# Splitting the evacuation of a products' bank, and a context in two column groups, in a two-layer metaformer kernel

## The chip, the cores and the metric

The kernel runs on one core of one Trainium2 chip. The metric is the device time of one execution in microseconds. Of the kernel before, three executions took 1307.3, 1311.6 and 1318.2 us, median 1311.6. One further execution was taken with the hardware profiler; all rows and durations below come from that one.

## The reference, cut to what matters

The input is x, 16 samples of 128 channels on 32 x 32 positions (1024 tokens), all in float32. Layer 0 adds linear attention and then a spectral filter (STU); layer 1 adds a pair of 3x3 convolutions and then a soft mixture of 64 experts. The change touches two places in layer 0: the attention's context, and the products of the spectral filter.

```python
q = jax.nn.softmax(q, axis=-2) * SCALE          # 4 heads of 32
k = jax.nn.softmax(k, axis=-1)
context = jnp.einsum('bhdc,bhec->bhde', k, v)
out = jnp.einsum('bhde,bhdc->bhec', context, q)
...
U_plus = jnp.fft.irfft(Vf[None, :, :, None] * Uf_p[:, :, None, :], n=n, axis=1)[:, :sl]
out = jnp.einsum('btkd,k,kde->bte', U_plus, s, Mpp)
out = out + jnp.einsum('btkd,k,kde->bte', U_minus, s, Mpm)
```

The second is a causal convolution over the 128 channels (the sequence of the filter is the channel axis) with 16 filters, each followed by a matrix; the same is done with a sign-alternated input. The kernel does it in the frequency domain: for every frequency it forms complex matrices G from filter spectra and mixed matrices, and multiplies the samples' spectra by it.

## The kernel before, in words

**Attention (about 10 to 395 us).** The work of a sample is cut into some 60 named steps. A table `period` lists the steps with a lag in samples, so that each pass over the table does steps of up to seven samples; this order is kept as written for TensorE, VectorE, ScalarE and GpSimd (a manual schedule pins these four; SP, which issues most DMAs, is ordered by the compiler). The step `context` (L476) multiplies, for each of 8 token tiles, the transposed exponentials of q (128 tokens x 128) by the scaled exponentials of k (128 x 128), and sums over the tiles in one PSUM tile `pc` of 128 x 128 (L482). All pairs of the four heads are computed, and `context_mask` (L488, VectorE) multiplies the result by a scale and a mask that keeps the four 32 x 32 blocks on the diagonal. Then `fold` and `fold2` combine it with output and value weights. PSUM tiles of a sample's 1024 numbers per partition come from `big`, three buffers. `moments` (L132) takes statistics of such a tile on VectorE; `tokens_copy` (L361), `input_copy` (L530) copy it to SBUF on ScalarE. `class_copy` (L232, L234) copies the upper half of a tile, `class_sums` and `class_differences` (L241, L248, L254) read its lower half on VectorE.

**Generation and products (about 395 to 676 us).** Frequencies are worked on in 16 chunks (NCH) of 8 (JL), with 128 columns each (CW). Two things happen per chunk:

- *Generation* of G for the next chunk, `generate(c, q)` (L774), in 8 parts q: each fills four PSUM banks, `pg[0]` to `pg[3]`, one for each group r of 32 rows, with four matrices of 128 columns. `collect` copies the four banks into the SBUF tile `g`, one bank per instruction, on VectorE (L785) or ScalarE (L787).
- *Products* with the present chunk, `multiply(c, m, x, py, fresh)` (L798): for each of four classes m and both halves x, 16 small matmuls write `py[:, x]`. `py` is one PSUM bank of 2 x 2 x 128 numbers per partition: x = 0 fills the first 256, x = 1 the second.

A float32 matmul appears as two TensorE instructions in the profile, so a generation part is 32 instructions and one half x of the products is 32.

The generations, the copies and the products of one m form a block; four blocks form a chunk. In a block, TensorE generates two parts (2m and 2m + 1) and then multiplies both halves. ScalarE then copies the whole bank `py` to the SBUF tile `yt` (L859), which has a single buffer. `combine` (L826, L827) adds and subtracts the two halves in SBUF on VectorE; it is called one block later, between the copies of the first part and those of the second. After the last class, `finish` (L812 to L815, GpSimd, in the last chunk VectorE) combines the classes and stores them (L819, SP). `begin(c)` (L765, L766 on GpSimd, loads L762 on SP) prepares the samples' spectra `v` of a chunk; it is called for the next chunk in the block m = 0, after `combine`.

`pg` and `py` share one pool, `psg`, of eight banks taken in turn. A block takes nine: four, four, one. So a block's `py` takes the bank that its own first `pg[0]` had, and the last bank of the next block's second generation is the one that `py` had.

**Convolutions and experts (about 688 us to the end).** Not touched.

Of the kernel before, what the change touches and what calls it, by code (L numbers as in the profile page):

```python
# [8 lines left out]
F32 = mybir.dt.float32  # L9
AF = mybir.ActivationFunctionType  # L10
ALU = mybir.AluOpType
# [3 lines left out]
P = 128  # L15
B, C, H, W = 16, 128, 32, 32
N = H * W
NT = N // 128
# [14 lines left out]
NCH = 16  # L33
JL = 8
# [6 lines left out]
RG = P // KR  # L41
# [25 lines left out]
def metaformer_kernel(ctx: ExitStack, tc: tile.TileContext, io: dict, out: bass.AP):  # L67
    nc = tc.nc
# [26 lines left out]
    for n, (g_, b_, m_, v_) in enumerate(((V_G1, V_B1, V_M1, V_V1), (V_G2, V_B2, V_M2, V_V2))):  # L95
# [15 lines left out]
                name=nc.get_next_instruction_name(), ins=[], outs=[], act_func_set_id=EXP_LN  # L111
# [52 lines left out]
    with ExitStack() as l0:  # L164
# [43 lines left out]
        with ExitStack() as a0:  # L208
# [8 lines left out]
            ps = a0.enter_context(tc.tile_pool(name="aps", bufs=2, space=PSUM))  # L217
# [97 lines left out]
            mask = aconst.tile([P, P], F32, name="mask")  # L315
            nc.vector.memset(mask, 0.0)
            for h in range(HEADS):
                s = slice(h * DH, (h + 1) * DH)
# [22 lines left out]
            class Attention:  # L341
# [134 lines left out]
                def context(self):  # L476


                    self.pc = ps.tile([P, P], F32, name="pc", tag="s")
                    ket = self.ke.rearrange("p (j h) d -> p j (h d)", h=HEADS)  # L480
                    for j in range(NT):
                        nc.tensor.matmul(  # L482
                            self.pc, self.qt[:, j, :], ket[:, j, :], start=(j == 0), stop=(j == NT - 1)
                        )

                def context_mask(self):
                    self.cx = work.tile([P, P], F32, name="cx", tag="cx")
                    nc.vector.scalar_tensor_tensor(  # L488
                        self.cx, self.pc, self.qs[:, 2:3], mask, ALU.mult, ALU.mult
                    )  # L490

                def fold(self):
# [253 lines left out]
        with ExitStack() as g0:  # L746
            gpl = [g0.enter_context(tc.tile_pool(name=f"gpl{i}", bufs=1)) for i in range(2)]
            cpl = g0.enter_context(tc.tile_pool(name="cpl", bufs=2))
# [5 lines left out]
            def begin(c):  # L754

                v = cpl.tile([P, 2 * NM * JL, 3, B], F32, name="v", tag="v")
                vs[c] = v
                vv = v.rearrange("p (x w) k b -> p x k b w", x=2)
                for i in range(B // BP):
                    bs = slice(i * BP, (i + 1) * BP)  # L760
                    xc = xcl.tile([P, BP, 2, 2, NM * JL], F32, name="xc", tag=f"xc{i}")
                    nc.sync.dma_start(xc.rearrange("p b x r w -> p b (x r w)"), vd[c, :, bs, :])  # L762
                    e, o = (xc[:, :, x].rearrange("p b r w -> p r b w") for x in range(2))
                    for x, op in enumerate((ALU.add, ALU.subtract)):
                        nc.gpsimd.tensor_tensor(vv[:, x, 1:, bs], e, o, op)  # L765
                    nc.gpsimd.tensor_scalar(v[:, :, 0, bs], v[:, :, 2, bs], -1.0, None, ALU.mult)  # L766
# [9 lines left out]
                        )  # L776
                return pg

            def collect(c, q, pg):

                for r in range(RG):
                    dst = gs[c].rearrange("p w (g q i) -> p g q w i", g=RG, q=NB)[:, r, q]
                    src = pg[r].rearrange("p i w -> p w i")
                    if r % 2 and (r == 1 or q % 4):
                        nc.vector.tensor_copy(dst, src)  # L785
                    else:
                        nc.scalar.copy(dst, src)  # L787

            def multiply(c, m, x, py, fresh):

                g, v = gs[c], vs[c]
                for kl in range(JL // RG):
                    for ri in range(2):
                        for grp in range(RG):
                            jl = RG * kl + grp
                            rows = slice(grp * 2 * B, (grp + 1) * 2 * B)

                            nc.tensor.matmul(  # L798
                                py[rows, x, kl, :],
                                v[:, (x * NM + m) * JL + jl, 1 - ri : 3 - ri, :]  # L800
                                .rearrange("p k b -> p (k b)"),
                                g[:, ((x * 2 + ri) * NM + m) * JL + jl, :],
                                start=(grp not in fresh), stop=(ri == 1), skip_group_check=True,
                            )
                            fresh.add(grp)
# [15 lines left out]
                        ys[:, kl].rearrange("p x m e -> p (x m e)"),  # L821
                    )

            def combine(c, m, ys, t):

                nc.vector.tensor_tensor(ys[:, :, 0, m], t[:, 1], t[:, 0], ALU.add)  # L826
                nc.vector.scalar_tensor_tensor(  # L827
                    ys[:, :, 1, m], t[:, 1], -1.0, t[:, 0], ALU.mult, ALU.add
                )
                if m == NM - 1:  # L830
                    finish(c, ys)

            with tc.manual_schedule(engines=PINNED):
                begin(0)
                gs[0] = gpl[0].tile([P, CW, C], F32, name="g", tag="g")
                for q in range(NB):
                    collect(0, q, generate(0, q))
                waiting = None
                for c in range(NCH):
                    if c + 1 < NCH:  # L840
                        gs[c + 1] = gpl[(c + 1) % 2].tile([P, CW, C], F32, name="g", tag="g")

                    ys = cpl.tile([P, JL // RG, 2, NM, C], F32, name="ys", tag="ys")
                    for m in range(NM):
                        if c + 1 < NCH:
                            pg = [generate(c + 1, 2 * m + x) for x in range(2)]
                            collect(c + 1, 2 * m, pg[0])
                        if waiting:
                            combine(*waiting)
                        if c + 1 < NCH:  # L850
                            if m == 0:
                                begin(c + 1)
                            collect(c + 1, 2 * m + 1, pg[1])
                        py = psg.tile([P, 2, JL // RG, C], F32, name="py", tag="p")
                        fresh = set()
                        for x in range(2):
                            multiply(c, m, x, py, fresh)
                        t = cpl.tile([P, 2, JL // RG, C], F32, name="yt", tag="yt", bufs=1)
                        nc.scalar.copy(t, py)  # L859
                        waiting = c, m, ys, t  # L860
                combine(*waiting)


    gpool = ctx.enter_context(tc.tile_pool(name="gpool", bufs=1))
# [9 lines left out]
    with ExitStack() as c1:  # L874
# [6 lines left out]
        ps = cps.enter_context(tc.tile_pool(name="cps", bufs=2, space=PSUM))  # L881
# [559 lines left out]
        with tc.manual_schedule(engines=PINNED):  # L1441
            hs, og = {}, {}
# [29 lines left out]
        ps = c1.enter_context(tc.tile_pool(name="fps", bufs=4, space=PSUM))  # L1472
        with tc.manual_schedule(engines=PINNED):
            for pr in (7, *range(NPAIR - 1)):
                py = [ps.tile([P, N], F32, name=f"pfy{j}", tag="pfy") for j in range(2)]
# [7 lines left out]
                for j in range(2):  # L1483
                    b = 2 * pr + j
                    if j and pr % 2:
                        t = first.tile([P, N], F32, name="yt", tag="v", bufs=2)
# [133 lines left out]
```

## Time and profile before

| | us |
|---|---|
| median of three executions | 1311.6 (1307.3 to 1318.2) |
| the profiled execution | 1324.2 |
| its span | 1322.4 |
| TensorE busy | 1209.1 (91%) |
| VectorE busy | 932.7 (71%) |
| ScalarE busy | 715.7 (54%) |
| GpSimd busy | 517.0 (39%) |
| chain that ended last: L774 | 9.1% of the span |
| chain: L798 | 8.2% |
| chain: L482 (context) | 2.2% |

In the rows, PE is TensorE, PEld its weight loads, DVE is VectorE, ACT ScalarE, POOL GpSimd, SP SyncE; L and a number is a line of the kernel. "us, us" in a timeline are the start from the span's beginning and the duration of a merged run of equal instructions; "xN" is how many. In brackets stands how long the engine had been idle before it and what ended that: an instruction of another engine, a DMA, or "issue", when nothing in the profile shows a reason. The chain of waits follows, from the last instruction back, what each step was released by. Shares of busy time are means over very different stages; what an edit in one stage is worth has to be read from that stage.

### The profile page before, as it was taken

To read this page: it belongs to the slowest core of one execution; us is meant where nothing else is said; L and a number is where in the kernel's file an instruction comes from. 1 tells how busy PE (TensorE), PEld (TensorE's weight loads), DVE (VectorE), ACT (ScalarE), POOL (GpSimd) and SP (SyncE) were. 2 spreads that over 40 slices of the span, in tenths; PEclk is the share of its full clock that TensorE was granted. 3 is DMA by queue.
4 is the path that set the end of the run, shared out by engine and by line. 5 is a ranking of instruction groups with operands and counts; after the bars stand their busy time and mean duration, and the time that the engine had idled before them with its cause. 6 is when DMAs were issued, how large, how long until landed. Compare 5 with 4: busy or idle time off the path is not lost.

```text
span 1322.4 us, 33679 instructions
## 1 busy us (share of the span) xinstructions
PE 1209.1 (91%) x14116; PEld 996.3 (75%) x14116; DVE 932.7 (71%) x1982; ACT 715.7 (54%) x1424; POOL 517.0 (39%) x816
## 2 busy tenths in 40 slices
PE   4889999999998999999938999999999999996875
PEld 3777777777767898898837988989889898872433
DVE  5688787887765778888747777777878777662224
ACT  3777777777546667666703345554545464652111
POOL 2324545454685888888832222121212121100002
PEclk8899999999998999999968999999999999995997
DMA  6014343433344333444375310312212113035986
GB/s 268 17 35 141 116 137 108 147 121 126 116 148 140 125 128 132 131 131 131 108 260 145 96 49 23 90 53 60 64 49 65 33 49 128 17 122 198 357 311 255
DMA packets 87400, 162.98 MB, mean 123 GB/s; under 512 B 5584, under 2 KB 40784, under 8 KB 86864
## 3 DMA queue, kind: packets, MB, share of 16 engines
q1 hardware_dynamic: 86608, 158.33, 36.1%
q0 software_dynamic: 640, 2.49, 0.6%
q8 instruction: 111, 1.82, 0.6%
q14 instruction: 41, 0.34, 0.1%
HBM read 104.18 MB, written 56.62 MB: 122 GB/s over the span
## 4 chain that ended last, share of the span: by engine, by line
PE 83%; DVE 6%; DMA 3%; ACT 3%; POOL 2%; issue 1%; SPq 0%; POOLq 0%; ACTq 0%; DVEq 0%
PE pcv L945 25%; PE pg L774 9%; PE py L798 8%; PE big L618 6%; PE big L149 4%; PE big L159 4%; PE big L1058 4%; PE big L551 3%; PE big L418 2%; PE pc L482 2%; PE big L514 2%; PE big L436 2%; DVE bst L132 2%; PE big L1206 1%; PE ph L1400 1%
## 5 line engine op out<-in xcount | busy, mean ns | idle before, releaser
L945 PE MATMUL pcv<-v,cw 128*128 128x256 f32 x1536 | 342.9, 380 | 0.0
L945 PEld LDWEIGHTS pcv<-v,cw 128*128 128x128 f32 x1536 | 286.8, 190 | 42.2 <-issue 5.7
L785 DVE COPY g<-pg 128x512 f32<-128x512 f32 x224 | 144.4, 682 | 60.6 <-PE pg L774 60.1
L787 ACT COPY g<-pg 128x512 f32<-128x512 f32 x288 | 147.3, 604 | 32.2 <-PE pg L774 32.1
L774 PE MATMUL pg<-ph,mst 32*128 32x128 f32 x4096 | 143.8, 279 | 4.1 <-issue 2.3
L774 PEld LDWEIGHTS pg<-ph,mst 32*128 32x128 f32 x4096 | 129.1, 186 | 19.8 <-issue 8.9
L798 PE MATMUL py<-g,v 128*32 128x128 f32 x4096 | 127.6, 276 | 9.3 <-POOL v L765 5.6
L798 PEld LDWEIGHTS py<-g,v 128*32 128x32 f32 x4096 | 110.1, 111 | 18.1 <-POOL v L765 5.8
L141 ACT ACTIVATE tok<-tok,sts 128x128 f32<-128x128 f32 x256 | 101.8, 481 | 23.8 <-POOL sts L1020 20.4
L132 DVE BATCH_NORM_STATS2 bst<-big 128x6 f32<-128x256 f32 x256 | 91.2, 418 | 19.1 <-PE big L154 12.1
L765 POOL TENSOR_TENSOR v<-xc 128x256 f32<-128x256 f32 x128 | 99.5, 801 | 9.3 <-DVE g L785 9.3
L1085 POOL TENSOR_SCALAR sts<-bst 128x8 f32<-128x8 f32 x16 | 6.5, 404 | 233.8 <-DVE bst L132 233.8
L939 DVE TENSOR_TENSOR v<-pads 128x544 f32<-128x544 f32 x128 | 85.0, 724 | 9.7 <-ACT pads L1138 9.3
L618 PE MATMUL big<-u,mu 128*128 128x128 f32 (+4 forms) x384 | 86.0, 380 | 0.0
L274 POOL TENSOR_TENSOR xf<-ab 128x256 f32<-128x256 f32 x34 | 24.8, 728 | 132.2 <-DVE ab L241 132.1
L859 ACT COPY yt<-py 128x512 f32<-128x512 f32 x64 | 37.5, 585 | 65.9 <-PE py L798 44.4
L618 PEld LDWEIGHTS big<-u,mu 128*128 128x128 f32 x384 | 56.7, 191 | 18.0 <-issue 15.4
L1116 ACT ACTIVATE ct<-pcv,bn 128x256 f32<-128x256 f32 x64 | 30.2, 473 | 69.3 <-PE pcv L945 68.4
L551 PE MATMUL big<-wf,ub 128*128 128x256 f32 x256 | 62.0, 385 | 0.2
L1134 DVE TENSOR_TENSOR r<-pcv,cs 128x256 f32<-128x256 f32 x64 | 27.0, 421 | 48.9 <-PE pcv L945 48.2
L149 PEld LDWEIGHTS big<-ident,x 128*128 128x128 f32 x384 | 47.3, 148 | 17.8 <-issue 7.2
L149 PE MATMUL big<-ident,x 128*128 128x128 f32 x384 | 53.8, 286 | 6.7 <-ACT tok L141 2.4
(231 smaller groups left out, 2341.5 us busy)
## 6 DMA issues: line engine op xcount, KB each, us to landing
we<-in_weight SPq DMA_DIRECT2D x32, 1024.0 KB, 11.1
vd<-xf SPq DMA_DIRECT2D x16, 1024.0 KB, 5.1
xc<-vd SPq DMA_DIRECT2D x64, 256.0 KB, 3.3
yd<-ys SPq DMA_DIRECT2D x32, 512.0 KB, 4.1
y<-yd SPq DMA_DIRECT2D x15, 896.0 KB, 6.5
x<-in_x SPq DMA_DIRECT2D x16, 512.0 KB, 4.1
mi<-in_M_phi SPq DMA_DIRECT2D x16, 512.0 KB, 5.0
xd<-x SPq DMA_DIRECT2D x16, 512.0 KB, 6.0
```

What stands on the lines that cost most here:

```text
L132: nc.vector.bn_stats(bst[:, j : j + 2, :].rearrange("p j s -> p (j s)"), src[:, j : j + 2, :].rearrange("p j c -> p c j"),)
L141: nc.scalar.activation(dst[:, j, :], src[:, j, :], AF.Identity, bias=nm[:, j : j + 1], scale=r[:, j : j + 1],)
L149: nc.tensor.transpose(pt[:, j, :], src[:, j * P : (j + 1) * P], ident)
L551: nc.tensor.matmul(dst, self.ub[:, q, :], wf[:, q, :], start=True, stop=True)
L618: nc.tensor.matmul(self.pa[:, a:hi], mu[:, NF - 1 - si, tap, :], self.u[:, a - tap : hi - tap], start=(tap == 0), stop=(tap == KU - 1),)
L765: nc.gpsimd.tensor_tensor(vv[:, x, 1:, bs], e, o, op)
L774: nc.tensor.matmul(pg[r][:, i], mst[rs, 4 * q + i, :], ph[rs, c, :], start=True, stop=True,)
L785: nc.vector.tensor_copy(dst, src)
L787: nc.scalar.copy(dst, src)
L798: nc.tensor.matmul(py[rows, x, kl, :], v[:, (x * NM + m) * JL + jl, 1 - ri : 3 - ri, :] .rearrange("p k b -> p (k b)"), g[:, ((x * 2 + ri) ...
L939: nc.vector.tensor_tensor(v[:, k], d[i], d[j], op)
L945: nc.tensor.matmul(pc[:, i], wt[:, dy, k, :], v[:, k, hf * HR + dy : hf * HR + dy + HR], start=(dy == 0), stop=(dy == 2),)
```

## The change

In the attention, the context is no longer 8 matmuls of 128 x 128 but 16: for each token tile, one for heads 0 and 1 (rows and columns 0 to 63) and one for heads 2 and 3 (64 to 127). Their outputs lie on partitions 0 to 63 and 64 to 127 of a PSUM tile of 128 x 64. The mask step reads that tile twice by a broadcast, so that the masked result has the same 128 x 128 numbers.

In the product stage,

- ScalarE copies only the first half of `py` (x = 0), between the two halves of the products, into a smaller `yt` with two buffers; the sums read the second half from PSUM;
- the sums of a block are issued at its own end, not in the next block;
- the copies of the generated banks alternate strictly: r = 0 and 2 on ScalarE, 1 and 3 on VectorE (before, ScalarE also had r = 3 for the parts 0 and 4);
- the copies of r = 2 and 3 of the second part are issued after the products;
- `begin` of the next chunk is called at the start of the chunk.

```diff
-                    self.pc = ps.tile([P, P], F32, name="pc", tag="s")
+                    self.pc = ps.tile([P, P // 2], F32, name="pc", tag="s")
...
                     for j in range(NT):
-                        nc.tensor.matmul(
-                            self.pc, self.qt[:, j, :], ket[:, j, :], start=(j == 0), stop=(j == NT - 1)
-                        )
+                        for g in range(2):
+                            hs = slice(g * P // 2, (g + 1) * P // 2)
+                            nc.tensor.matmul(
+                                self.pc[hs, :], self.qt[:, j, hs], ket[:, j, hs],
+                                start=(j == 0), stop=(j == NT - 1), skip_group_check=True,
+                            )
...
                     nc.vector.scalar_tensor_tensor(
-                        self.cx, self.pc, self.qs[:, 2:3], mask, ALU.mult, ALU.mult
+                        self.cx.rearrange("p (g e) -> p g e", g=2),
+                        self.pc.unsqueeze(1).to_broadcast([P, 2, P // 2]), self.qs[:, 2:3],
+                        mask.rearrange("p (g e) -> p g e", g=2), ALU.mult, ALU.mult,
                     )
...
-            def collect(c, q, pg):
+            def collect(c, q, pg, rs=range(RG)):
-                for r in range(RG):
+                for r in rs:
...
-                    if r % 2 and (r == 1 or q % 4):
+                    if r % 2:
                         nc.vector.tensor_copy(dst, src)
                     else:
                         nc.scalar.copy(dst, src)
...
-            def combine(c, m, ys, t):
-                nc.vector.tensor_tensor(ys[:, :, 0, m], t[:, 1], t[:, 0], ALU.add)
+            def combine(c, m, ys, py, t):
+                nc.vector.tensor_tensor(ys[:, :, 0, m], py[:, 1], t, ALU.add)
                 nc.vector.scalar_tensor_tensor(
-                    ys[:, :, 1, m], t[:, 1], -1.0, t[:, 0], ALU.mult, ALU.add
+                    ys[:, :, 1, m], py[:, 1], -1.0, t, ALU.mult, ALU.add
                 )
...
-                waiting = None
                 for c in range(NCH):
-                    if c + 1 < NCH:
+                    more = c + 1 < NCH
+                    if more:
                         gs[c + 1] = gpl[(c + 1) % 2].tile([P, CW, C], F32, name="g", tag="g")
+                        begin(c + 1)
                     ys = cpl.tile([P, JL // RG, 2, NM, C], F32, name="ys", tag="ys")
                     for m in range(NM):
-                        if c + 1 < NCH:
+                        if more:
                             pg = [generate(c + 1, 2 * m + x) for x in range(2)]
                             collect(c + 1, 2 * m, pg[0])
-                        if waiting:
-                            combine(*waiting)
-                        if c + 1 < NCH:
-                            if m == 0:
-                                begin(c + 1)
-                            collect(c + 1, 2 * m + 1, pg[1])
+                            collect(c + 1, 2 * m + 1, pg[1], range(2))
                         py = psg.tile([P, 2, JL // RG, C], F32, name="py", tag="p")
+                        t = cpl.tile([P, JL // RG, C], F32, name="yt", tag="yt")
                         fresh = set()
-                        for x in range(2):
-                            multiply(c, m, x, py, fresh)
-                        t = cpl.tile([P, 2, JL // RG, C], F32, name="yt", tag="yt", bufs=1)
-                        nc.scalar.copy(t, py)
-                        waiting = c, m, ys, t
-                combine(*waiting)
+                        multiply(c, m, 0, py, fresh)
+                        nc.scalar.copy(t, py[:, 0])
+                        multiply(c, m, 1, py, fresh)
+                        if more:
+                            collect(c + 1, 2 * m + 1, pg[1], range(2, RG))
+                        combine(c, m, ys, py, t)
```

## The prediction

> **What bounds the kernel now.** I read the page first, then the stage the change edits, then the second edit's place. The page's slices give the engine and the stages:
>
> ```profile
> PE   4889999999998999999938999999999999996875
> PEclk8899999999998999999968999999999999995997
> ```
>
> TensorE is nine tenths busy nearly everywhere. At 33.1 us a slice, slices 3 to 11 are attention and slices 12 to 20 (about 395 to 690 us) generation and products; the clock is full in both. The timeline of TensorE shows what a product block costs (one step of m: two generations, L774, then the products, L798):
>
> ```profile
> 545.44 2.07 PE L774 MATMUL pg<-ph,mst 32*128 32x128 f32 x64
> 547.44 1.95 PE L798 MATMUL py<-g,v 128*32 128x128 f32 x64
> 549.33 2.07 PE L774 MATMUL pg<-ph,mst 32*128 32x128 f32 x64
> ...
> 643.89 1.95 PE L798 MATMUL py<-g,v 128*32 128x128 f32 x64
> ...
> 659.75 1.96 PE L798 MATMUL py<-g,v 128*32 128x128 f32 x64
> 663.15 7.19 PE L798 MATMUL py<-g,v 128*32 128x128 f32 x256 [1.45 <-DVE pooled L868]
> ```
>
> An undisturbed block is 549.33 - 545.44 = 3.89 us: 2.00 generation, 1.89 products. The 60 blocks that start from 418.02 to 657.75 take 243.6 us (to 659.75 + 1.89), 4.06 each. So 0.17 x 60 = 10.2 us is all that faster evictions could return there; 3.4 of it are five TensorE gaps with no releaser ("issue", 1.06, 0.40, 0.45, 0.18 and 1.28 us), which I leave in place. 6.8 us can be won.
>
> The groups of instructions, shapes apart, give the engines that empty PSUM (count | busy us, mean ns | idle before):
>
> ```profile
> L787 ACT COPY g<-pg 128x512 f32<-128x512 f32 x288 | 147.3, 604 | 32.2 <-PE pg L774 32.1
> L785 DVE COPY g<-pg 128x512 f32<-128x512 f32 x224 | 144.4, 682 | 60.6 <-PE pg L774 60.1
> L827 DVE SCALAR_TENSOR_TENSOR ys<-yt 128x256 f32<-128x256 f32 x64 | 48.3, 755 | 0.0
> L859 ACT COPY yt<-py 128x512 f32<-128x512 f32 x64 | 37.5, 585 | 65.9 <-PE py L798 44.4 <-DVE ys L827 10.7 <-ACT g L787 8.5
> L826 DVE TENSOR_TENSOR ys<-yt 128x256 f32<-128x256 f32 x64 | 36.1, 565 | 4.4 <-POOL pads L924 2.2 <-ACT yt L859 2.2
> L361 ACT COPY tok<-big 128x1024 f32<-128x1024 f32 x16 | 16.2, 1013 | 14.9 <-DVE bst L132 5.4 <-PE big L149 4.8 <-PE pc L482 3.4
> ```
>
> Per block VectorE needs 3.5 x 682 + 565 + 755 = 3.7 us and ScalarE 4.5 x 604 + 585 = 3.3, both under 4.06: TensorE sets the pace. In attention the chain of waits shows one sample:
>
> ```profile
> 191.75 1.79 PE pc L482 x16
> ...
> 195.32 1.44 DVE bst L132 x4
> ...
> 196.84 1.02 ACT ub L530
> ...
> 197.90 1.09 PE big L159 x8
> ```
>
> The context, 1.79 us, lies on the path of every sample. The timeline shows what orders that ACT copy:
>
> ```profile
> 196.84 1.01 ACT L530 COPY ub<-big 128x1024 f32<-128x1024 f32 x1 [2.21 <-DVE bst L132]
> ...
> 206.18 0.60 ACT L234 ACTIVATE et<-big 128x512 f32<-128x512 f32 x1 [2.33 <-DVE ab L241]
> ```
>
> L530 and the bn_stats of L132 both only read the same PSUM tile, yet the copy starts when the statistics end. L234 reads the upper half of a tile (`pe[:, 2:]`) and L241 the lower half, and it too waits. Accesses to one PSUM tile by two engines are put one behind the other here, even reads of different halves.
>
> **The product block, part by part.** *The wait that is added.* The products' tile `py` is one bank of 512 numbers per partition. Now its first half is copied by ScalarE between the two halves of the products. By the two rows above, the second half's writes are queued behind that copy. TensorE then stands with nothing else to issue: its 32 instructions of x=1 wait, behind them the next block's generation, and behind that the copies of both evicting engines. The price: products are (1.95 - 0.27) / 63 = 26.7 ns apart (0.27 us is one instruction), so the last of the first 32 starts at 0.83 and ends at 1.10. ScalarE starts 0.11 later (products end at 645.84, the next L859 begins at 645.95). The copy of 256: from 585 ns for 512 and 1013 for 1024, 0.836 ns an element, so 0.37; bounds 0.31 (L118, 8 elements wide, 310 ns) and 0.47 (L1116, an ACTIVATE of 256 from PSUM, 473 ns). TensorE starts 0.05 after a ScalarE copy (L530 ends 197.85, L159 starts 197.90). Sum 1.63, where the second half used to start at 32 x 26.7 = 0.85: a stall of 0.78, bounds 0.72 and 0.88. ScalarE is free in time: its three earlier copies start 1.2, 1.7 and 2.2 after the block and end by 2.8, the half is ready at 2.00 + 1.10 = 3.10.
>
> The Trainium skill, "PSUM — Partial Sum Buffer", section "PSUM bank collisions raise a hardware error", speaks against this edit: guard PSUM by bank and quadrant, not by address, because two engines in one bank at once collide even at different columns. The trace agrees, with the waits of 2.21 and 2.33 us above; by address alone the sum would be that of the first rival below.
>
> *The sums.* L826 and L827 had two SBUF operands and ran 0.40 to 1.97 us beside a busy GpSimd. They now take one from PSUM, as L625 does in attention, whose 16 instances beside GpSimd stay between 1.224 and 1.226 us. L1124 and L1125 have this shape with one PSUM operand: 419 and 413 ns. I take 0.77 for the pair (672.00 to 672.77 undisturbed). It is now at the block's end, ahead of the next block's VectorE copies: it starts at 2.00 + 1.63 + 1.10 + 0.11 = 4.84 and ends at 5.61, while the next block starts at 3.89 + 0.78 = 4.67, its first copies at 4.67 + 1.2 = 5.9. The bank it frees is needed by the fourth tile of that block's second generation, at 4.67 + 1.00 + 0.19 = 5.86. It costs nothing, with 0.2 us to spare.
>
> *The evictions.* 32 copies go from ScalarE to VectorE. VectorE then has 4 x 682 + 770 = 3.5 us, ScalarE 4 x 604 + 371 = 2.8, of 4.67. The 6.8 us of bank stalls go, since these come from the sums pushing L785 back. ScalarE's third copy of the second generation, now behind the half copy, ends at 3.57 + 0.6 = 4.2; its bank is needed at 5.7: hidden.
>
> *The moved start of the next values* (GpSimd L765, L766 and four loads on SP). Order on GpSimd and SP is as before: last chunk's L812 to L815 and its stores, then these. GpSimd has 4.2 + 10.2 = 14.4 us of work in a chunk that grows to 18.7; it stays hidden.
>
> Sum: 60 x (3.89 + 0.78) + 3.4 = 283.6 against 243.6, +40.0. First block +0.8. Last chunk, four blocks of products only, +3.1. The wait of 1.5 us ahead of it (661.64 to 663.15, for GpSimd's values) goes: -1.5. Behind the last product, today's backlog of single-buffered copies and sums ends 6.0 us later (670.34 to 676.38); now 0.11 + 0.77 and L812 to L815 on VectorE (674.17 to 676.38, 2.2) make 3.1: -2.9. Stage: **+39.5**.
>
> **The context.** 16 instructions 112 ns apart become 32 with half the columns, in two column groups. Nearest row:
>
> ```profile
> 835.59 1.97 PE L1261 MATMUL pp<-tt,gtt 128*64 128x128 f32 x32
> ```
>
> Two groups of 64, 128 moving columns: (1.97 - 0.27) / 31 = 54.8 ns apart. Around it TensorE loses 0.10 in front (835.59 less 832.90 + 12 x 0.216) and 0.15 behind (837.49 less 835.59 + 32 x 0.0548), 0.25 in all, which a plain context doesn't pay. Lower bound: the products' 26.7 ns, 32 x 0.0267 + 0.25 = 1.10, -0.69. Upper bound: 54.8 stays, if loading weights sets it: 2.00, +0.21. I take half of 54.8, 27.4 ns, since L1261's spacing is that of its moving columns shared by two groups (L945 shows 216 ns per 256): 1.13, -0.66. The bn_stats wait behind moves along with TensorE (it idles 0.75 for L154). 14 of the 16 samples are on the path; the first two run into a wait of 2.88 us for VectorE (74.48). **-9.2**; at the upper bound +2.9.
>
> The page "TensorE: Matmul & The Clock Gate" ("LDWEIGHTS") gives columns / 1.2 ns for a weight load, 53 ns for 64, and in its Part 3 lets loads overlap running matmuls only across row groups; by that the context would take 32 x 0.053 + 0.25 = 1.96 us, about +2.3 in all. The products' 26.7 ns, across column groups, don't decide it, as their loads are 32 wide.
>
> The mask (L488, 351 ns) keeps its element count.
>
> **Total**: +39.5 - 9.2 = +30.3. On the profiled execution, 1324.2 us (span 1322.4), that is 1354.5; on the median of the runs, 1311.6, it is **1342**. With the upper bound for the context, 1354.
>
> **Rivals.**
> 1. *No wait in mid-block: faster.* If dependencies are kept by address, x=1 runs on. Then 6.8 + 1.5 + 2.9 us return and the context's 9.2: -20, **1291**. For it: the halves don't overlap. Against: L234, whose half doesn't overlap either. It decides if the stall is under about 0.3 us (0.3 x 65 = 20).
> 2. *VectorE becomes the bound as well.* If the sums still stretch to 0.95 each beside GpSimd, the pair ends at 4.84 + 1.6 = 6.4, 0.6 past the 5.86 at which the bank is needed: 60 x 0.6 = +36 more, **1378**. Against: L625.
> 3. *The context doesn't overlap*: **1354**, still slower.
>
> **How the numbers follow.** Forecast 0.50; rival 3, 0.32; rival 1, 0.09; rival 2, 0.05; between forecast and rival 1, 0.04. About 1% is what a measurement tells from no change (1298 to 1325). Faster by over 1%: 0.09. Within: 0.05. Slower: 0.86. Forecast and rival 3 alone, with stalls of 0.72 to 0.88 us over 65 blocks (-4, +7) and the 3.4 us of gaps hidden or not, reach from 1335 to 1361; the run spread (1307 to 1318) adds some 5 each way. Range 1326 to 1366.
>
> **What would show it.** Right: every L798 run split in two groups of 32 with 0.7 to 0.9 us of TensorE idle between, released by ACT's yt copy; blocks 4.6 to 4.8 us apart; L826 and L827 near 0.42 us; TensorE about 83% busy at full clock there (as at 60 to 80 us, 15.98 of 20 us, clock 1.00). Context: 32 instructions in 1.1 to 1.2 us. Wrong: 64 products without a gap (rival 1); gaps inside L774 released by VectorE (rival 2); a context of 2 us (rival 3); a clock below full in the stage, which I haven't priced.

## The result, and the profile after

| | before | after |
|---|---|---|
| median of four executions, us | 1312.6 (1307.3 to 1318.2) | 1353.6 (1350.2 to 1358.9) |
| ratio, 95% interval | | 1.0298 (1.0261 to 1.0334) |
| the profiled execution, us | 1324.2 | 1350.8 |
| its span, us | 1322.4 | 1349.1 |

The change costs 41 us in the medians, 26.7 us between the spans of the two profiled executions. Every ratio in this document is against executions of the kernel before that were taken along; their median was 1312.6 us here and 1315.8 to 1317.3 us beside the experiments, so ratios compare better than microseconds. The lines have moved by five (generation is L779 now, products L803), the sums are L831 and L832, the context is L484.

The page's slices of the changed kernel, TensorE's busy share and granted clock:

```profile
PE   4889999999978888888883999999999999996886
PEclk9999999999999999999996899999999999997998
```

In slices 13 to 19 (counted from 0), all of the product stage, TensorE's share has fallen from 9 to 8, at a granted clock of 1.00 (413 to 690 us): TensorE stands, it isn't slowed. The timeline of one block with its second half, sums and half copy shows where:

```profile
540.01 2.23 PE L779 MATMUL pg<-ph,mst 32*128 32x128 f32 x64
540.22 0.42 DVE L831 TENSOR_TENSOR ys<-py,yt 128x256 f32<-128x256 f32 x1 [1.28 <-PE py L803]
540.56 0.41 DVE L832 SCALAR_TENSOR_TENSOR ys<-py,yt 128x256 f32<-128x256 f32 x1
...
542.17 1.08 PE L803 MATMUL py<-g,v 128*32 128x128 f32 x32
543.37 0.37 ACT L859 COPY yt<-py 128x256 f32<-128x256 f32 x1 [0.60 <-ACT g L792]
...
543.79 1.08 PE L803 MATMUL py<-g,v 128*32 128x128 f32 x32 [0.54 <-ACT yt L859]
...
544.80 2.32 PE L779 MATMUL pg<-ph,mst 32*128 32x128 f32 x64
```

The products' run of 64 has become two of 32. Between them lie 0.54 us that ScalarE's copy of `yt` ends. The first 32 start at 542.17, the second at 543.79, so the products take 2.63 us to the next generation at 544.80, where they took 1.89. The generation, too, is longer: 2.16 us from 540.01 to 542.17, where an undisturbed one took 2.00. The block is 544.80 - 540.01 = 4.79 us, which is also the median of the stage, against 3.89 undisturbed before. The average before was 4.13: the 243.6 us that the prediction divides by 60 hold 59 blocks (more on this below).

The waits in the stage, summed (us in total, times, longest):

```profile
PE py L803 <- ACT yt L859: 32.3, 60, 0.8
...
PE pg L779 <- issue: 2.2, 4, 1.1
```

Sixty waits for the half copy, one in each block with a generation. The groups of the copies show how long their engines now stand:

```profile
L792 ACT COPY g<-pg 128x512 f32<-128x512 f32 x256 | 139.0, 592 | 116.7 <-PE pg L779 115.5
...
L790 DVE COPY g<-pg 128x512 f32<-128x512 f32 x256 | 159.4, 684 | 18.9 <-PE pg L779 18.6
```

ScalarE stood 32.2 us ahead of these copies before and stands 116.7 now. VectorE's idle time has moved: 60.6 us ahead of its copies before and 18.9 now, but now 62.6 us ahead of the sums, for the products. In the stage, ScalarE's busy share fell from 68% to 50% and VectorE's from 78% to 66%: both have room that nobody uses, since TensorE feeds them more slowly.

In attention, the chain of waits of the changed kernel for the sample that was shown before:

```profile
185.41 1.08 PE pc L484 x32
186.49 1.02 PE big L159 x8
...
188.43 1.44 DVE bst L132 x4
...
189.95 1.02 ACT ub L535
```

Before, the line behind the context was:

```profile
193.53 0.87 PE big L159 x8
```

The context has gone from 1.79 to 1.08 us with twice the instructions. The transposes behind it (L159) went from 0.87 to 1.02, so the sample gains 0.56.

The timeline of TensorE at the end of the stage:

```profile
708.12 1.08 PE L803 MATMUL py<-g,v 128*32 128x128 f32 x32 [0.54 <-ACT yt L859]
723.32 1.20 PE L1060 MATMUL big<-wi,y 128*128 128x128 f32 x4 [14.12 <-DMA y<-yd]
```

The wait between last product and first convolution product is 14.12 us; it was 17.34.

To compare runs I cut each profiled span at four events that every kernel has: the first context product, the first generation, the last product of the spectral filter, the first product of the convolutions.

| us | to context | attention | stage | wait behind it | rest |
|---|---|---|---|---|---|
| before | 55.1 | 340.2 | 275.1 | 17.3 | 634.7 |
| after | 52.5 | 332.3 | 324.4 | 14.1 | 625.8 |
| difference | -2.6 | -7.9 | +49.3 | -3.2 | -8.9 |

The change touches the middle three: +38.2 us. The first and the last column hold work that no kernel here alters, and they vary from execution to execution: over the twelve profiles of this study the first runs from 51.7 to 55.5, the last from 625.8 to 636.7. In the one of before, the granted clock was 0.84 from 5 to 35 us and 0.96 over 600 us of the last part; in the one of after 0.90 and 0.97. That profile of before was a long execution of its kernel, which is why the spans show less than the medians do.

### The profile page after: what moved, and what is told of

The parts are those of the page before. It is cut to its first block, busy times and chain, and to the rows that moved or that the text cites. A ratio compares the mean times of both kernels' runs of the same rounds, so it can differ in the third digit from the quotient of the medians.

```text
span 1349.1 us, 34300 instructions
## 1 busy us (share of the span) xinstructions
PE 1208.9 (90%) x14372; PEld 982.7 (73%) x14372; DVE 925.0 (69%) x2014; ACT 687.7 (51%) x1392; POOL 505.2 (37%) x816
## 4 chain that ended last, share of the span: by engine, by line
PE 81%; DVE 5%; ACT 5%; DMA 3%; issue 3%; POOL 1%; SPq 0%; POOLq 0%; ACTq 0%; DVEq 0%
PE pcv L947 24%; PE pg L779 10%; PE py L803 8%; PE big L623 6%; PE big L159 4%; PE big L149 4%; PE big L1060 4%; PE big L556 3%; PE big L436 2%; PE big L418 2%; PE big L519 2%; DVE bst L132 2%; ACT yt L859 2%; PE big L1208 1%; PE pp L1263 1%
## 5 line engine op out<-in xcount | busy, mean ns | idle before, releaser
L792 ACT COPY g<-pg 128x512 f32<-128x512 f32 x256 | 139.0, 592 | 116.7 <-PE pg L779 115.5
L803 PE MATMUL py<-g,v 128*32 128x128 f32 x4096 | 139.5, 278 | 41.9 <-ACT yt L859 34.5
L790 DVE COPY g<-pg 128x512 f32<-128x512 f32 x256 | 159.4, 684 | 18.9 <-PE pg L779 18.6
L803 PEld LDWEIGHTS py<-g,v 128*32 128x32 f32 x4096 | 105.2, 110 | 67.2 <-ACT yt L859 51.9
L779 PE MATMUL pg<-ph,mst 32*128 32x128 f32 x4096 | 148.7, 281 | 4.0 <-issue 2.2
L779 PEld LDWEIGHTS pg<-ph,mst 32*128 32x128 f32 x4096 | 135.6, 187 | 18.3 <-issue 17.7
L770 POOL TENSOR_TENSOR v<-xc 128x256 f32<-128x256 f32 x128 | 91.3, 738 | 9.8 <-DMA xd<-x 9.8
L831 DVE TENSOR_TENSOR ys<-py,yt 128x256 f32<-128x256 f32 x64 | 27.2, 425 | 98.7 <-PE py L803 67.7
L623 PEld LDWEIGHTS big<-u,mu 128*128 128x128 f32 x384 | 56.7, 191 | 18.0 <-issue 15.4
L1118 ACT ACTIVATE ct<-pcv,bn 128x256 f32<-128x256 f32 x64 | 30.3, 474 | 67.5 <-PE pcv L947 66.6
```

The source lines that it names most:

```text
L623: nc.tensor.matmul(self.pa[:, a:hi], mu[:, NF - 1 - si, tap, :], self.u[:, a - tap : hi - tap], start=(tap == 0), stop=(tap == KU - 1),)
L779: nc.tensor.matmul(pg[r][:, i], mst[rs, 4 * q + i, :], ph[rs, c, :], start=True, stop=True,)
L803: nc.tensor.matmul(py[rows, x, kl, :], v[:, (x * NM + m) * JL + jl, 1 - ri : 3 - ri, :] .rearrange("p k b -> p (k b)"), g[:, ((x * 2 + ri) ...
```

## The experiments

Two things needed a cause: the gap in mid-products, and the 0.16 us by which the generation had grown, which I hadn't foreseen. For the gap the theory (A in the expectations) is that the second half's writes wait for a copy out of the same bank; the rival is that 32 small matmuls with a gap are simply how this split runs. For the generation the theory (B in the expectations) is that the bank which the sums release comes too late for the generation's last tile; the rival is that generation became slower for a reason of its own, such as VectorE reading PSUM beside it. A third cause came up in the first runs, late instruction fetches (C).

**One bank for each half (e1).** Each half gets a tile of its own, and with it a bank of its own; products and sums address `py[0]` and `py[1]`. Against the changed kernel:

```diff
-                        py = psg.tile([P, 2, JL // RG, C], F32, name="py", tag="p")
+                        py = [psg.tile([P, JL // RG, C], F32, name="py", tag="p") for x in range(2)]
...
-                        multiply(c, m, 0, py, fresh)
-                        nc.scalar.copy(t, py[:, 0])
-                        multiply(c, m, 1, py, fresh)
+                        multiply(c, m, 0, py, set())
+                        nc.scalar.copy(t, py[0])
+                        multiply(c, m, 1, py, set())
```

> The changed kernel with the two halves of the products in two PSUM banks instead of one. Theory A (the second half's products are queued behind ScalarE's copy because both are in one bank): the 0.54 us TensorE gap in the middle of every products run vanishes, 64 products run in 1.95 us again, a block takes 2.16 + 1.89 = 4.05 us instead of 4.79; over 60 blocks -44 us, with the last chunk -46: about 1307 us, ratio to the kernel before 0.995 (0.99 to 1.00). The generation's 0.16 us over 2.00 stays (theory B: its last tile waits for the bank that the sums free). Rival (the gap comes from splitting the products into two runs, or from ScalarE being late, not from the shared bank): the gap stays, 1345 to 1360 us, ratio about 1.03.

Measured: 1327.7 us (1320.2 to 1331.3), ratio 1.0077 (1.0043 to 1.0111). The timeline of that kernel, TensorE and one half copy:

```profile
545.83 1.95 PE L803 MATMUL py<-g,v 128*32 128x128 f32 x64
547.02 0.37 ACT L858 COPY yt<-py 128x256 f32<-128x256 f32 x1 [0.60 <-PE py L803]
...
547.71 2.40 PE L779 MATMUL pg<-ph,mst 32*128 32x128 f32 x64
...
550.04 1.95 PE L803 MATMUL py<-g,v 128*32 128x128 f32 x64
...
551.92 1.61 PE L779 MATMUL pg<-ph,mst 32*128 32x128 f32 x45
...
554.41 0.93 PE L779 MATMUL pg<-ph,mst 32*128 32x128 f32 x19 [0.88 <-issue]
```

With the same copy at the same place, 64 products run in 1.95 us without a gap. So the gap comes from what the two halves shared, and not from the split: that is shown. Whether it is the bank or the tile isn't: e1 separates both at once, and a tile of two banks wasn't tried. A row of the prediction points at the tile: L234 reads the second 512 numbers of a tile of 1024 and L241 the first 512, so by the 512 numbers of a bank they read different banks, and yet L234 waited 2.33 us for L241.

The time didn't follow: the ratio is 1.0077 where 0.995 was expected, some 17 us more. The last line shows the kind of thing that ate it: TensorE stops inside a generation and no engine and no semaphore released it. Between the starts of two matmuls inside generations there are 22 gaps of over 0.25 us in this run, 17.3 us in all, where the kernel before had 10 with 5.4 and the changed one 8 with 4.8. What they follow is told with e7.

**The half copy behind both halves, one bank (e2).** Against the changed kernel:

```diff
                         multiply(c, m, 0, py, fresh)
-                        nc.scalar.copy(t, py[:, 0])
                         multiply(c, m, 1, py, fresh)
+                        nc.scalar.copy(t, py[:, 0])
```

> The changed kernel with ScalarE's copy of the first half issued after both halves of the products, still one bank. Theory A: no gap inside the products. Theory B (the generation is stretched because the bank of the products is freed only when both sums have read it): the sums now end about 0.42 us later, 1.38 us after the generation's start instead of 0.96, so the generation grows from 2.16 to about 2.6 us, all of it at the fourth tile of its second part; block 4.5 us, 60 x -0.3 = -18 and the last chunk -3: about 1333 us, ratio 1.015. Rival to B (the generation's 0.16 us has another cause, for instance evictions on both engines at once): the generation stays at 2.16, block 4.05, about 1309 us, ratio 0.997.

Measured: 1340.3 us (1338.2 to 1344.7), ratio 1.0193 (1.0167 to 1.0218). The timeline of that kernel:

```profile
571.39 1.95 PE L803 MATMUL py<-g,v 128*32 128x128 f32 x64
...
573.27 2.71 PE L779 MATMUL pg<-ph,mst 32*128 32x128 f32 x64
573.45 0.37 ACT L860 COPY yt<-py 128x256 f32<-128x256 f32 x1 [1.58 <-PE py L803]
...
573.86 0.42 DVE L831 TENSOR_TENSOR ys<-py,yt 128x256 f32<-128x256 f32 x1 [1.24 <-ACT yt L860]
574.20 0.41 DVE L832 SCALAR_TENSOR_TENSOR ys<-py,yt 128x256 f32<-128x256 f32 x1
...
575.91 0.32 PE L803 MATMUL py<-g,v 128*32 128x128 f32 x4
```

The products are whole again. The sums now wait for the copy and end at 574.61, 1.34 us into the generation, which grows to 2.64 (575.91 - 573.27; median of the run 2.60). The stall has moved from the products into the generation: the later the bank is released, the longer the generation. That is what B says. It is also why a copy at the end is no repair by itself: the block is 4.48 us. The ratio was expected at 1.015; this run, too, has more gaps without a releaser, 18 with 13.2 us.

**The second sum without the bank (e6).** The second sum is formed in SBUF as twice the first half less the first sum, so that the bank is free after the first sum; the result is the same difference, rounded otherwise. Against the changed kernel:

```diff
                 nc.vector.scalar_tensor_tensor(
-                    ys[:, :, 1, m], py[:, 1], -1.0, t, ALU.mult, ALU.add
+                    ys[:, :, 1, m], t, 2.0, ys[:, :, 0, m], ALU.mult, ALU.subtract
                 )
```

> The changed kernel with the second sum taken from SBUF, as twice the copied half less the first sum, so that only the first sum reads the products' bank. Theory B (the last tile of the next generation waits, with its weight load, for the bank that both sums hold until 0.96 us into the generation; without a wait that load would start at about 0.9): the bank is free at 0.63, the generation falls from 2.16 to 2.00 us, the block from 4.79 to 4.63, 60 x -0.16 = -9.6: about 1344 us, ratio 1.023. The second sum, now with both operands in SBUF, may stretch to 0.95 us beside GpSimd; VectorE has room for it. Rival (another cause of the 0.16): the generation stays at 2.16, 1353, ratio 1.030.

Measured: 1341.9 us (1338.5 to 1344.4), ratio 1.0191 (1.0146 to 1.0236). Its timeline:

```profile
545.29 2.07 PE L779 MATMUL pg<-ph,mst 32*128 32x128 f32 x64
545.50 0.42 DVE L831 TENSOR_TENSOR ys<-py,yt 128x256 f32<-128x256 f32 x1 [1.03 <-PE py L803]
...
545.96 0.95 DVE L832 SCALAR_TENSOR_TENSOR ys<-yt,ys 128x256 f32<-128x256 f32 x1
...
547.29 1.08 PE L803 MATMUL py<-g,v 128*32 128x128 f32 x32
```

The generation is back at 2.00 us (547.29 - 545.29), though VectorE works beside it for longer than before, and the block at 4.62. So the 0.16 us was the bank's release and not VectorE's presence. The ratio fell by 0.0107, which is 14 us, where 9.6 were expected: the gaps without a releaser fell as well, from 4.8 us to one of 0.4, which I hadn't foreseen and which no run explains. With two SBUF operands the second sum stretches (0.95 us here, up to 1.47), and it costs nothing, since no bank hangs on it.

**The half copy twice (e5).** The line `nc.scalar.copy(t, py[:, 0])` stands twice in a row. One execution.

> The changed kernel with ScalarE's half copy done twice in the middle of the products (the second writes the same values). Theory A: TensorE's gap grows by one more copy, about 0.31 us (373 ns copies overlap by some 60 ns), in all 64 blocks: +20 us on the changed kernel, a block of 5.1 us, about 1373 us. Rival (TensorE does not wait for ScalarE's copy): the gap stays 0.54 us and the time 1350 to 1359.

Measured: 1378.9 us in its one execution. Its timeline:

```profile
546.22 0.37 ACT L859 COPY yt<-py 128x256 f32<-128x256 f32 x1 [0.65 <-PE py L803]
546.62 0.37 ACT L860 COPY yt<-py 128x256 f32<-128x256 f32 x1
...
547.05 1.08 PE L803 MATMUL py<-g,v 128*32 128x128 f32 x32 [0.90 <-ACT yt L860]
```

TensorE's gap grows from 0.54 to 0.90 us, by one copy, and it starts 0.06 us after the second copy's end. The copy's whole duration is part of the wait, nothing of it is absorbed.

**The context alone (e3), and the product stage alone (e4).** e3 is the kernel before with only the context and its mask changed; e4 is the changed kernel with the old context and mask.

> The kernel before with only the context in two column groups. If the two groups overlap as the changed kernel's trace shows (32 instructions in 1.08 us where 16 took 1.79, the next group 0.15 longer): -0.56 us a sample, 14 samples on the path, -8 us: about 1304 us, ratio 0.994. If the changed kernel's 10 us at the end of attention were something else: 1312, ratio 1.000.

> The changed kernel with the old context of 128 x 128: the product stage's part of the change alone. If the two parts add up: 1353.6 + 8 = 1362 us, ratio 1.037 (1.033 to 1.040). If the context's gain is lost or doubled beside the new product stage, 1354 or above 1368.

Measured: e3 1306.9 us (1302.9 to 1312.6), ratio 0.9937 (0.9917 to 0.9957); e4 1364.0 us (1359.3 to 1371.8), ratio 1.0361 (1.0293 to 1.0428). The chain of e3 has the same steps as that of the changed kernel:

```profile
185.42 1.08 PE pc L484 x32
186.50 1.02 PE big L159 x8
```

Attention takes 332.3 us in e3, and 340.8 in e4. So the parts add up: the context alone is a gain of 0.6%, the product stage alone a loss of 3.6%.

**The start of the next values put back (e10).** Against the changed kernel, `begin(c + 1)` goes back behind the sums of the block m = 0:

```diff
-                        begin(c + 1)
-
...
                         combine(c, m, ys, py, t)
+                        if more and m == 0:
+                            begin(c + 1)
```

> The changed kernel with the next chunk's spectra begun behind the sums of the first block instead of at the chunk's start. GpSimd's order is the same either way (last chunk's combination, then these), and it has 14.4 us of work in a chunk of 19: no change, 1350 to 1358 us, ratio 1.03. If the earlier call mattered to SP's loads or to when the spectra are ready, TensorE waits for GpSimd's v ahead of a chunk's products would appear and the time grow by 1 to 3 us a chunk, 15 to 40 in all.

Measured: 1357.9 us (1352.3 to 1364.8), ratio 1.0329 (1.0287 to 1.0371), beside 1.0298 (1.0261 to 1.0334). No difference that these runs can tell, and no wait of TensorE for GpSimd's values appears ahead of the later chunks' products, where one would have shown.

**The stores apart (e7).** The gaps of e1 come after late instruction fetches. In the DMA records one queue of instructions moves pieces of 16 KB, 63 of them in the stage of e1, about one for each block; with the weight loads a block has 256 instructions of TensorE, so I take these pieces for TensorE's. From the DMA records of the trace of e1, with the generation gap that follows:

```
fetch at   interval   stores issued before it   moved in the 2 us before   TensorE resumes, gap
500.18     5.15 us    3.42 and 3.06 us          373 GB/s                   502.38, 0.68
517.49     5.55       3.55 and 3.18             367                        519.79, 0.87
534.67     5.31       3.42 and 3.05             383                        537.07, 1.01
552.07     5.54       3.54 and 3.17             365                        554.41, 1.15
```

The gap column runs from one matmul's start to the next, so 1.15 here is the 0.88 of idle time in the timeline above. The usual interval is 4.36 us. Of the fourteen fetches in e1's stage that came more than 5 us after the one before, twelve follow the two stores of 512 KB of a finished chunk by 3.0 to 4.3 us, and each of the twelve is followed by a gap. In the kernel before, the stores lie 4.9 to 7.0 us ahead of the late fetches, 154 to 202 GB/s move in the 2 us before, and only four of eight are followed by a gap. If the stores delay the fetch, issuing them one block apart should remove most gaps. Against e1, `finish` of a chunk only notes its two stores, and ScalarE issues one each in two later blocks (the last two chunks store as before):

```diff
+                        if m in (1, 2) and done:
+                            store(nc.scalar, *done.pop(0))
                         combine(c, m, ys, py, t)
```

> The two-bank version with the two 512 KB stores of a chunk issued apart by ScalarE, behind the copies of the second and the third block of the next chunk, instead of together by SP. Theory C (the TensorE gaps without releaser, 14 in the two-bank trace, 0.6 to 1.7 us and about one a chunk, come from TensorE's instruction fetches of 16 KB, which arrive 5.1 to 6.2 us apart instead of 4.1 where one falls 3.0 to 4.3 us behind the issue of 1 MB of stores): with half the bytes at a time the late fetches are later by less than the fetch's lead, the gaps fall from 17 us in all to under 7; 1328 becomes about 1317, ratio 1.000. Rival (the gaps follow something else in the chunk, as the four loads of the next spectra): they stay at about one a chunk, 1328, ratio 1.008.

Measured: 1318.7 us (1313.7 to 1324.1), ratio 1.0015 (0.9990 to 1.0039). The gaps fell from 17.3 to 11.2 us where under 7 was expected. The time fits, and part of the gaps did go with the stores issued apart and by another engine; that it is by way of the fetch is argued, and what makes the remaining gaps isn't settled. Late fetches are still there, some near a single store, some near none. Leaving the stores or the loads of the spectra out altogether wasn't tried.

**All together (e8).** Two banks, the second sum in SBUF, the stores apart, the context in two groups: every cost that had been found, taken out.

> Two banks, the second sum from SBUF and the stores apart, with the context in two groups. If theories A, B and C hold, a block takes 3.89 to 4.0 us with few gaps: 60 x (4.06 - 3.95) = 7 us under the kernel before in the blocks, 3 at the end of the stage, 8 in attention, about 1297 us, ratio 0.987. If a faster TensorE meets the next limit at once (fetches, or VectorE's sums stretched by GpSimd), it stays near the kernel with the context alone: 1305 to 1312, ratio 0.994 to 0.999.

Measured: 1314.8 us (1309.1 to 1319.8), ratio 0.9984 (0.9958 to 1.0009). The first expectation, 0.987, failed; the ratio lies in the range of the second, 0.994 to 0.999, in which a faster TensorE meets the next limit at once (in us, 1314.8 is above both, but the kernel before took 1317.3 beside it). Its timeline has the block that the change was built for, and right behind it a part of what takes it back:

```profile
546.40 2.07 PE L779 MATMUL pg<-ph,mst 32*128 32x128 f32 x64
548.40 1.95 PE L803 MATMUL py<-g,v 128*32 128x128 f32 x64
550.28 2.06 PE L779 MATMUL pg<-ph,mst 32*128 32x128 f32 x62
552.50 0.38 PE L779 MATMUL pg<-ph,mst 32*128 32x128 f32 x2 [0.16 <-issue]
```

The first block is 550.28 - 546.40 = 3.88 us, the undisturbed one of before. In the next, TensorE stops two instructions before the generation's end. The 59 blocks take 243.3 us, as they did before (243.4), and the stage 274.3 (275.1). Gaps inside generations are 5.8 us of that, hardly more than the 5.4 before; the rest is spread over longer generations and products, whose causes weren't followed. The wait behind the stage is 19.2 us, longer than before. So even in this form the product stage returns nothing. Of the context's gain (attention took 332.9 us here) 1.8 us are lost in that wait; the untouched last part took 636.7 us in this profile, the longest of the study, and why that is so stays open.

**The last chunk's sums early (e9).** On e3, the best so far, the sums of the last chunk are issued in their own block:

```diff
                         waiting = c, m, ys, t
+                        if c + 1 == NCH:
+                            combine(*waiting)
+                            waiting = None
```

> The kernel before with the context in two groups, and in the last chunk alone (where nothing is generated) the sums issued right behind each block's copy instead of one block later. The backlog of single-buffered copies and sums behind the last product (6.0 us in the kernel before) becomes one copy, one pair of sums and the last combination, 0.1 + 0.6 + 0.8 + 2.2 = 3.7 us: -2.3 on the kernel with the context alone, about 1304 us, ratio 0.992. If the stores, and not the sums, set when the convolutions start: no change, 0.9937.

Measured: 1306.0 us (1301.9 to 1320.3), ratio 0.9938 (0.9903 to 0.9974), the same as e3. The wait behind the stage fell from 17.2 to 15.4 us, and the stage itself was longer in that profile (279.9 against 273.2), with more gaps of TensorE that no release explains. No gain can be claimed. e3 and e9 are the versions that beat both kernels, by 0.6% against the kernel before, and e3 is the simpler one.

## Why the prediction held, and where a step was wrong

It gave 1342 us, slower, between 1326 and 1366; measured were 1353.6. That this lies beside rival 3's 1354 is chance: rival 3 is a context that doesn't overlap, and it does. By its own steps:

- **The wait that is added: right.** Predicted were 1.63 us from the first half's start to the second's, a stall of 0.78; measured 1.62, and 0.75 more for the products. The copy was put at 0.37 and measured 0.37. Rival 1, an order by address, fell. The rule of the Trainium skill, "PSUM — Partial Sum Buffer", section "PSUM bank collisions raise a hardware error", to guard by bank and not by address, fits the gap (0.54 us with one bank, none with two in e1). But e1's halves are also two tiles, and the 2.33 us of L234, which the prediction counts for the rule, lie between the two banks of one tile: they speak for an order by whole tiles, of which the rule says nothing. Two of the signs were misput: TensorE's idle time was given as 0.7 to 0.9 us and its busy share as 83%, where the prediction's own sum leaves 1.63 - 1.10 = 0.53 us idle; measured are 0.54 us and 88%.
- **The sums: duration right, their price wrong.** The changed kernel's records of the two (minimum, median and maximum in ns):

```profile
L831 DVE TENSOR_TENSOR ys<-py,yt x64: 423/425/426, 409.1 to 709.3; 128x256 f32<-128x256 f32 x64
L832 DVE SCALAR_TENSOR_TENSOR ys<-py,yt x64: 411/414/425, 409.4 to 709.7; 128x256 f32<-128x256 f32 x64
```

  No instance is stretched beside GpSimd, so rival 2's mechanism fell. The sums end 0.96 us into the next generation; 0.94 was predicted. The step of the prediction that failed is the one after it: "It costs nothing, with 0.2 us to spare." I had let the fourth tile of the second part want its bank at 1.00 + 0.19 us. The starts in the trace say otherwise. In ns from the generation's start, around the second part's first matmuls (before: the generation at 545.44):

```
before   weight loads   886  893  899  906      matmuls   995 1002 1008 1015
after    weight loads   886  892  899  997      matmuls   995 1002 1008 1107
```

  The four row groups start together, 7 ns apart, and the weight load runs 0.11 us ahead of its matmul. The bank was wanted at 0.91 us, the sums ended at 0.96, and the load that waited started at 1.00. TensorE waits there some 0.1 us and ends the generation with stragglers; 2.16 instead of 2.00 us. Sixty times 0.16 is 9.6 us. e6 took the cause away and had 2.00, e2 made it worse and had 2.60. This is the wait that rival 2 describes, a generation that stands for the bank of the sums, by another cause and at a quarter of its 0.6 us.
- **The evictions: right.** Where no bank of the sums holds TensorE, in e6, the generations take 2.00 us in the median and 2.02 in the mean, against 2.12 and 2.20 before: the old stalls are gone.
- **The stage: a block miscounted.** Predicted +42.4 with the first block, the last chunk and the wait that goes, measured +49.3. The sum sets 60 blocks of the changed kernel against 243.6 us before, which hold only 59: from 418.02 to 657.75 the kernel before starts 59 generations, 4.13 us a block, and the first block's generation lies in the run before them. With 59 on both sides the prediction's own terms give 42.4 - 4.7 = +37.7. The 11.6 us that are then missing are 59 x 0.16 = 9.4 for the bank, less 59 x 0.03 = 1.8 for the smaller stall, and some 4 for gaps and other irregular blocks: the 59 blocks took 290.1 us, 7.5 more than 59 x 4.79, where 3.4 had been kept.
- **The end of the stage: right**, -3.2 for -2.9.
- **The moved start: right** that it is hidden (e10).
- **The context: right in mechanism, a little too large.** 1.13 us with the switches was predicted; measured are 1.08 and 0.15 in the transposes behind. 14 samples at 0.56 are 7.8 us, and attention got 7.9 us shorter, where -9.2 was written. Rival 3 fell. The 1.96 us that the prediction works out from the page "TensorE: Matmul & The Clock Gate" ("LDWEIGHTS" and Part 3) count 32 loads of 64 columns one behind the other, since that part lists loads as overlapping running matmuls only where the row group differs (it names a background buffer for weights too, which the prediction left out). The trace contradicts the 1.96: 1.08 us, with the loads of the two column groups starting in pairs 7 ns apart, a pair every 55 to 59 ns.

The sum in the three touched parts is +38.2 where +30.3 was predicted, and +25.6 with the blocks counted right, which makes 1337 us and not 1342. So the error in the count hid 4.7 us of what was missing; by luck the forecast was nearer than its working. The medians differ by 41.0; the 2.8 us between this and 38.2 lie within what the untouched parts vary.

## What to carry to other kernels

When an instruction reads part of a PSUM tile while TensorE still has to write the rest, the whole handover (end of the matmuls, copy, release) goes onto TensorE's path, 0.75 us a time here; give the parts tiles in banks of their own, or read only when the tile is complete and its bank isn't wanted soon. The moment at which a bank had to be free here wasn't the start of the matmul that writes it but that of its weight load, 0.11 us earlier, and with four row groups it was the start of the whole group: compute the slack from the loads. Where half of a full-width product is masked away afterwards, two column groups side by side can be worth the 0.15 us that the next transposes lose: the context was the only part of this change that paid, 0.6%.

## What the runs showed of the hardware

- Weight loads of 64 columns in two column groups start side by side, in pairs 7 ns apart: 32 instructions in 1.08 us, 34 ns each, where 16 of full width took 1.79. The next full-width transposes take 0.15 us longer.
- VectorE with one operand in PSUM and one in SBUF keeps its time beside GpSimd (411 to 426 ns over 128 instances); with both in SBUF the same shape ran from 424 to 1474 ns in e6.
- An instruction queue moves 16 KB about once a block, taken here for TensorE's. In e1, fetches that came 5.1 to 6.2 us after the one before, instead of 4.4, were followed by gaps of up to 1.7 us between the starts of two matmuls. The changed kernel, with blocks of 4.79 us, has late fetches too and few gaps (4.8 us in all). That slower blocks give the slack is argued, and the length of the block can't be all of it: e6 with 4.62 us has 0.4 us of gaps, e10 with 4.79 has 8.4. Issuing the stores apart took a third of e1's gaps away; the rest is open.
- The untouched last part took 625.8 to 636.7 us over the twelve profiles. Three had a granted clock of 0.96 over its first 600 us and took 631.3 to 634.7 us, eight had 0.97 or 0.98 and took 625.8 to 632.1; but the longest, 636.7 us in e8, had 0.97 as well, so the clock isn't all of it.
